# Layer 0 of an image and attention kernel: x for the residual goes into other places, and is biased and turned over at another point

## The chip, the cores and the metric

The kernel runs on one core of a Trainium2 chip. A core has five engines with a queue of instructions each: TensorE (PE; its weight loads are listed as PEld), VectorE (DVE), ScalarE (ACT), GpSimd (POOL) and SyncE (SP). SP issues most of the DMA transfers, which 16 DMA engines carry out. The metric is the device time of one execution in microseconds (us); lower is better. The kernel before took 2713.66 us (median of three runs, 2711.21 to 2717.59).

## The reference, cut to what matters

The input x is an image of 256 channels and 64 x 64 pixels, in float32. Layer 0 normalises it by groups of channels, and adds to x a linear attention over windows of the image. Layer 1, an attention over all pixels and a mixture of eight experts, isn't touched by the change.

```python
x = x + _L0_conv_ref(_gn(x), Wq, Wk, Wv, Wout, bout)      # layer 0

def _L0_conv_ref(x, Wq, Wk, Wv, Wout, bout):              # 8 heads of 32 channels
    q, k, v = projections of x by Wq, Wk, Wv
    q = sigmoid(q); k = sigmoid(k)
    v = v / maximum(norm(v, axis=channels of a head), 1e-12)
    Ik, Ikv = integral images of k and of k * v
    for w in (1, 2, 4):                                   # box of 64 / w pixels
        wk, wkv = _box(Ik, 64 // w), _box(Ikv, 64 // w)
        attn = (q . wkv) / (q . wk + 1e-06)
    return Wout @ concatenate(attn) + bout
```

The sum with x is the residual. The kernel keeps it in the tile `t`, with pixels on the partitions; x comes from memory with channels outermost, so it must be turned over on its way into `t`, and `bout` is added to it before that.

## The kernel before, in words

Layer 0 works on 4096 pixels in 32 tiles of 128 (NT = 32), ordered so that eight strips (NCH = 8) of eight columns hold four bands (NB = 4) of 16 rows each. The 256 channels are handled in two halves (KC = 2, the loop variable `g`): for each half `prepare` (from L393) makes keys, values, sums and queries, and `attend` (from L696) uses them. The change touches `prepare` for g = 0 and what stands ahead of it.

1. **Load and statistics.** Eight DMAs (L324) bring x; DVE takes its statistics (L343) and writes the normalised image to `act` (L358, eight instructions). Statistics, means and some constants lie in a small pool, `c_x`, that ends here.
2. **The rows for the residual.** L369 to L375: the tile `rows` takes the place of x (tag "qk"), so its DMAs wait until the last L358 has read x. Sixteen DMAs on SP's queue, of 256 KB each, load x again: four bands (`b`), each in four quarters (`q`). `biased(b)` (L377) adds `bout` on ACT, eight instructions a band (L379). `residual(b)` (L382) turns a band over on DVE into `t`, eight instructions of 32 x 32 blocks (L385).
3. **Keys and values.** The loop over `i4` (L436) makes eight groups of four tiles. In each: 16 matmuls into a pair of PSUM banks (L441; the trace lists 16 halves for 8 instructions of the program), a sigmoid on ACT into `kt` (L453), a copy on DVE into `v` (L454), squares on POOL (L455), their sums by head on DVE (L456). After the fourth and the eighth group, a square root on ACT (L459) and the normalisation of 16 tiles of `v` on DVE (L460 to L463). The pairs of banks are three in number, shared with the sums of cells. Sigmoid and square root lie in different tables of ACT, so each change loads a table (1.28 us).
4. **Sums of cells.** `sum_cells` (L407), four parts: small matmuls `kt` x `v` (L418) that need the normalised `v`; ACT copies them to the tile `st` (L430). The first two parts are emitted in the last two rounds of the loop, the other two in the next stage.
5. **Area and boxes.** A loop over eight strips `ix` (L530): matmuls of `kt` with a triangular constant (L534, L538), and additions on DVE (L543 to L548). Between them DVE does the steps of `near` (L486): running sums over `st` (L490, L493), then differences (`boxes`, L504 and L510) into tiles `half` and `ssum` for the widths 4 and 2.
6. **Queries and denominators.** `by_channel` (L471) projects queries and keys again by channel (L476), with a sigmoid on ACT (L483). For three widths DVE makes `tall` and `edge` (L583, L585) and the products with the queries (L597 to L604, in two product tiles of the pool's tag "st"), which PE sums (L608). L621 ends the stage, and `attend` follows.

What sets the order: the program's tile framework places the instructions of every engine in a fixed order when the program is built; each engine takes its own queue in that order and waits for semaphores of the others. `tc.issue_after(x)` says that the instructions inside may stand only behind x. Before the change the biasing and the turning over are placed like this:

```python
    if not g and i4 >= NT - 8:                               # groups 6 and 7: bands 0 and 1
        order.enter_context(tc.issue_after(biased((i4 - NT + 8) // 4)))
    ...
    if not g:                                                # after the loop
        biased(2)
        biased(3)
    ...
    if not g and 1 <= ix <= NB:                              # area strips 1 to 4
        with tc.issue_after(latest.ins):
            residual(ix - 1)
```

Of the kernel before, what the change touches and what calls it, by code (L numbers as in the profile page):

```python
# [22 lines left out]
F32 = mybir.dt.float32  # L23
BF16 = mybir.dt.bfloat16
I32 = mybir.dt.int32
AF = mybir.ActivationFunctionType
# [16 lines left out]
D = 32  # L43
GRP = 8
REACH = (4, 2, 1)
# [75 lines left out]
def tile_conv_attn_hybrid(ctx: ExitStack, tc: tile.TileContext, a: dict, out: bass.AP):  # L121
    nc = tc.nc
# [145 lines left out]
    with ExitStack() as phase:  # L268
# [9 lines left out]
        big = phase.enter_context(tc.tile_pool(name="c_big", bufs=1))  # L278
# [18 lines left out]
        with (  # L297
# [21 lines left out]
            x = big.tile([P, KC, N], F32, tag="qk", name="x")  # L319
            xr = a["x"].rearrange("(k p) n -> p k n", p=P)  # L320
            for i in range(4):
                for k in range(KC):
                    at = slice(i * N // 4, (i + 1) * N // 4)
# [42 lines left out]

        rows = big.tile([P, NB, C // D, 4 * IMG], F32, tag="qk", name="rows")  # L369
        for b in range(NB):  # L370
            for q in range(4):
                nc.sync.dma_start(
                    rows[D * q : D * (q + 1), b],
                    a["x"].rearrange("(j c) (b q f) -> b q c j f", c=D, b=NB, q=4)[b, q],
                )  # L375

        def biased(b):  # L377
            for j in range(C // D):
                last = nc.scalar.activation(rows[:, b, j], rows[:, b, j], AF.Identity, bias=bout[:, j : j + 1])  # L379
            return last.ins  # L380

        def residual(b):  # L382

            for i in range(NCH):
                last = nc.vector.transpose(  # L385
                    t[:, NB * i + b, :C].rearrange("p (j c) -> p j c", c=D),
                    rows[:, b].rearrange("p j (y i c) -> p j y i c", y=4, c=SW)[:, :, :, i, :],
                )
            return last.ins

# [2 lines left out]
        def prepare(g, w3, prep, ps):  # L393
# [8 lines left out]
            v = big.tile([P, NT, P], F32, tag="v", name="v")  # L402
            sq = prep.tile([P, NT, P], F32, tag="area", name="sq")
            heads = lambda z: z.rearrange("p i (h d) -> p (i h) d", d=D)
            st = prep.tile([P, NCH, SW, D], F32, tag="st", name="st", bufs=2)
            cells = []

            def sum_cells(part):

                if part % 2 == 0:  # L410
                    cells.append(two_banks())
                sp = cells[-1]
                for i in range(NT // 4 * part, NT // 4 * (part + 1)):
                    for u in range(2):
                        us = slice(CELL * u, CELL * (u + 1))
                        for h in range(4):
                            hs = slice(D * h, D * (h + 1))
                            nc.tensor.matmul(  # L418
                                sp[hs, u, D * (i % 16) : D * (i % 16 + 1)],
                                kt[us, i, hs],  # L420
                                v[us, i, hs],
                                start=True,
                                stop=True,
                                skip_group_check=True,
                            )
                if part % 2:
                    some = slice(NCH // 2 * (part // 2), NCH // 2 * (part // 2 + 1))
                    for u in range(2):
                        with tc.issue_after(rooted.ins):
                            nc.scalar.copy(  # L430
                                st[:, some].rearrange("p i (m u) f -> p i m u f", u=2)[:, :, :, u, :],
                                sp[:, u, :].rearrange("p (i m f) -> p i m f", m=NB, f=D),
                            )

            ss = prep.tile([P, 4 * NT], F32, name="ss")
            for i4 in range(0, NT, 4):  # L436
# [10 lines left out]
                        )  # L447
                at = slice(i4, i4 + 4)

                with ExitStack() as order:  # L450
                    if not g and i4 >= NT - 8:
                        order.enter_context(tc.issue_after(biased((i4 - NT + 8) // 4)))
                    nc.scalar.activation(kt[:, at, :], kv[:, :, 0, :], AF.Sigmoid)  # L453
                nc.vector.tensor_copy(v[:, at, :], kv[:, :, 1, :])  # L454
                nc.gpsimd.tensor_mul(sq[:, at, :], v[:, at, :], v[:, at, :])  # L455
                nc.vector.tensor_reduce(ss[:, 4 * i4 : 4 * (i4 + 4)], heads(sq[:, at, :]), AX.X, ALU.add)  # L456
                if i4 % 16 == 12:
# [5 lines left out]
                    unit_v = nc.vector.tensor_mul(to, to, ss[:, half].unsqueeze(2).to_broadcast([P, 2 * NT, D]))  # L463
                if i4 >= NT - 8:
                    sum_cells((i4 - NT + 8) // 4)

            if not g:
                biased(2)
                biased(3)

            def by_channel(n, i):  # L471

# [13 lines left out]
            def near():  # L486


                for i in range(1, NCH):
                    nc.vector.tensor_add(st[:, i], st[:, i], st[:, i - 1])  # L490
                    yield
                for i in range(1, SW):
                    nc.vector.tensor_add(st[:, :, i], st[:, :, i], st[:, :, i - 1])  # L493
                    yield

                def boxes(to, src, r, axis):
# [16 lines left out]

                for r in REACH[:2]:
                    half = prep.tile([P, NCH, SW, D], F32, tag="st", name="half", bufs=2)
                    boxes(half, st, r, 0)
                    yield
                    boxes(ssum[r], half, r, 1)
                    yield
# [10 lines left out]
            for ix in range(NCH):  # L530
# [18 lines left out]
                side, latest = upto, add  # L549
                if ix in (1, 2):  # L550
                    sum_cells(ix + 1)
                if not g and 1 <= ix <= NB:
                    with tc.issue_after(latest.ins):
                        residual(ix - 1)
                for _ in range(3 if ix > 1 else 0):
                    next(steps, None)
            for _ in steps:
# [1597 lines left out]
```

## Time and profile before

The page describes one profiled execution; the median of the runs comes from other executions of the same kernel.

| | |
|---|---|
| median of three runs | 2713.66 us (2711.21 to 2717.59) |
| the profiled execution's own time | 2709.02 us |
| its span, from first to last instruction | 2707.1 us |
| mean granted clock of TensorE | 0.99 |
| busy share of the span: PE, DVE, ACT, POOL | 97%, 69%, 56%, 30% |
| first preparation of layer 0 (from the first projection to L621) | 22.28 to 127.43 us |
| `rows` DMAs on SP's queue | 16 x 256 KB, issued 27.3 to 39.6 us |
| biasing (L379, ACT) | 32 instructions of 0.50 us, begun between 45.1 and 70.6 us |
| turning over (L385, DVE) | 32 instructions of 0.40 us, begun between 62.5 and 82.1 us |

How to read the views: a line of the order of time gives the start, the length, the engine, the line of the code, the operation, and what it writes and reads; "x8" means that eight such instructions are joined. In brackets stands how long the engine had been idle before and what it waited for. Lines joined this way overlap a little, since an engine starts an instruction before the one ahead has quite ended. A line of stretches gives start and end, the length, then the busy time of each engine with its number of instructions, the granted clock of TensorE, the busy share of the DMA engines and GB/s. The chain of work that ended last is followed back from the last instruction, at each step to what released it.

### The profile page before, as it was taken

What the parts mean: (1) busy time and instruction counts of PE and PEld (TensorE: products, weight loads), DVE (VectorE), ACT (ScalarE), POOL (GpSimd) and SP (SyncE); (2) the same over time, 40 slices, a digit from 0 to 9 for tenths busy, and PEclk for the clock granted to TensorE, in tenths of its full rate; (3) what the DMA queues carried; (4) which work ended last, traced back from release to release, by engine and by line L of the source; (5) the groups of instructions that cost most, each with busy time, mean ns of one, the idle gap of its engine ahead of it and who ended that gap; (6) DMA issues with size and microseconds to landing.
All of it is one profiled execution on the core that took longest, in us unless ns stands there. A gap on an engine that the chain in (4) does not pass through costs nothing.

```text
span 2707.1 us, 70743 instructions
## 1 busy us (share of the span) xinstructions
PE 2624.4 (97%) x30398; PEld 1221.8 (45%) x30398; DVE 1880.5 (69%) x2570; ACT 1518.1 (56%) x2079; POOL 817.9 (30%) x919
## 2 busy tenths in 40 slices
PE   6999999999999999999999999999999999999995
PEld 5465436746544654111212121212121278888884
DVE  6868788586878866888888889888888871111114
ACT  3342323234232435999898989898989842222222
POOL 2067777306777731010000100000001122222220
PEclk9899999999999999999999999999999999999996
DMA  5000000000000000555555555555556645555555
GB/s 148 7 19 26 10 29 22 12 13 23 26 9 31 22 22 13 113 115 118 110 114 114 118 109 118 105 118 118 126 114 151 153 142 197 173 200 170 191 175 196
DMA packets 114461, 256.56 MB, mean 95 GB/s; under 512 B 19890, under 2 KB 76440, under 8 KB 100052
## 3 DMA queue, kind: packets, MB, share of 16 engines
q0 software_dynamic: 22240, 132.66, 23.4%
q1 hardware_dynamic: 84724, 110.30, 12.5%
q10 hardware_dynamic: 7168, 8.92, 1.0%
q8 instruction: 242, 3.96, 0.6%
q14 instruction: 87, 0.71, 0.1%
HBM read 118.64 MB, written 17.86 MB: 50 GB/s over the span
## 4 chain that ended last, share of the span: by engine, by line
PE 91%; DVE 4%; DMA 3%; issue 1%; ACT 1%; POOL 0%; ACTq 0%; SPq 0%; DVEq 0%; POOLq 0%
PE ps_three L1860 19%; PE ps_acc L1819 19%; PE ps_sc L887 8%; PE ps_yp L1528 8%; PE ps_hp L1511 7%; PE ps_acc L903 7%; PE ps_sc L767 3%; PE ps_sc L797 3%; PE ps_acc L841 3%; PE ps_two L441 2%; PE ps_mm L1303 2%; DMA yrows<-v,qk 2%; PE ps_two L534 1%; PE ps_acc L816 1%; PE ps_three L1794 1%; PE ps_mm L1318 1%
## 5 line engine op out<-in xcount | busy, mean ns | idle before, releaser
L1860 PE MATMUL ps_three<-qk 32*64 32x512 f32 x6144 | 563.2, 612 | 2.3 <-DVE t L1798 1.3
L1860 PE MATMUL ps_one<-qk 32*64 32x512 f32 x2048 | 556.3, 613 | 0.2 <-ACT pe L1869 0.2
L1892 DVE TENSOR_TENSOR act<-act,pe 128x2048 f32<-128x2048 f32 x195 | 447.3, 2294 | 82.5 <-ACT pe L1872 51.6
L1872 ACT ACTIVATE pe<-ps_three 128x1536 f32<-128x1536 f32 x330 | 477.3, 1446 | 0.0
L651 ACT COPY sm<-ps_sc 128x384 f32<-128x384 f32 (+2 forms) x418 | 212.9, 539 | 452.4 <-PE ps_sc L887 323.0
L659 DVE TENSOR_TENSOR sm<-ps_sc,mask 128x512 f32<-128x512 f32 (+3 forms) x788 | 343.3, 499 | 64.7 <-PE ps_sc L887 62.3
L659 POOL TENSOR_TENSOR sm<-sm,mask 128x192 f32<-128x192 f32 (+4 forms) x444 | 349.9, 819 | 113.3 <-ACT sm L651 113.2
L1892 DVE TENSOR_TENSOR act<-act 128x2048 f32<-128x2048 f32 x150 | 343.8, 2292 | 51.4 <-ACT act L1872 37.9
L1880 POOL DMA_DIRECT2D pe<-pe x108 | 93.4, 865 | 939.8 <-ACT pe L1872 610.4
L1819 PE MATMUL ps_acc<-pe,v 128*32 128x512 f32 x2640 | 351.6, 604 | 0.0
L1514 ACT ACTIVATE v<-ps_hp,qk 128x256 f32<-128x256 f32 (+1 forms) x256 | 123.1, 481 | 342.6 <-PE ps_hp L1511 342.6
L1860 PEld LDWEIGHTS ps_three<-qk 32*64 32x64 f32 x6144 | 112.6, 129 | 414.5 <-ACT pe L1869 244.0
L1872 ACT ACTIVATE act<-ps_three 128x1536 f32<-128x1536 f32 x182 | 263.1, 1446 | 0.0
L1528 PE MATMUL ps_yp<-qk,v 128*128 128x256 f32 (+1 forms) x1088 | 241.7, 380 | 0.0
L1511 PE MATMUL ps_hp<-qk 128*128 128x256 f32 (+1 forms) x1024 | 236.8, 389 | 2.8 <-ACT v L1514 1.7
L887 PE MATMUL ps_sc<-qk 32*128 32x256 f32 (+5 forms) x3456 | 233.2, 445 | 0.1
L1869 ACT ACTIVATE pe<-ps_one 128x512 f32<-128x512 f32 x330 | 197.5, 598 | 58.3 <-PE ps_one L1860 33.8
L1528 PEld LDWEIGHTS ps_yp<-qk,v 128*128 128x128 f32 (+1 forms) x1088 | 200.3, 187 | 30.7 <-issue 1.3
L903 PE MATMUL ps_acc<-sm,v 128*32 128x256 f32 (+4 forms) x2816 | 211.7, 407 | 0.1
L659 POOL TENSOR_TENSOR sm<-sm,ycut 128x512 f32<-128x512 f32 (+3 forms) x130 | 144.4, 1133 | 214.0 <-ACT sm L651 213.7
L1511 PEld LDWEIGHTS ps_hp<-qk 128*128 128x128 f32 x1024 | 180.7, 189 | 52.7 <-ACT v L1514 12.8
L1819 PE MATMUL ps_acc<-act,v 128*32 128x512 f32 x1456 | 193.9, 604 | 0.0
(364 smaller groups left out, 2908.8 us busy)
## 6 DMA issues: line engine op xcount, KB each, us to landing
pe<-pe POOLq DMA_DIRECT2D x108, 1024.0 KB, 7.6
qk<-in_L_ffn_W SPq DMA_DIRECT2D x64, 1024.0 KB
by<-recs SPq DMA_DIRECT2D x48, 256.0 KB
rows<-in_x SPq DMA_DIRECT2D x16, 256.0 KB
qk<-in_L_ffn_b SPq DMA_DIRECT2D x32, 128.0 KB
y<-yrows SPq DMA_DIRECT2D x8, 512.0 KB
y<-yrows ACTq DMA_DIRECT2D x8, 512.0 KB
rec<-recs SPq DMA_DIRECT2D x60, 64.0 KB
```

The costliest lines, as they stand in the source:

```text
L651: copied = nc.scalar.copy(sm[:, :used], sc[:, :used])
L659: done = engine.tensor_mul(to, of, mk.unsqueeze(1).to_broadcast(list(to.shape)))
L887: nc.tensor.matmul(scs[h][u : u + rows, at : at + n], kT[hs[h], P * i + u : P * i + u + rows], qT[hs[h], CH * ix + CELL * c0 : CH * ix + C ...
L903: nc.tensor.matmul(acc[hs[h], CELL * c0 : CELL * c1], v[:, i, hs[h]], sms[h][:, at : at + n], start=not begun[0], stop=last and at == plac ...
L1511: nc.tensor.matmul(hp[:, :n], w1[:, k, tok(m)], x_now[:, k, :n], start=k == 0, stop=k == KC - 1)
L1514: done["gelu"] = nc.scalar.activation(hid[:, m, :n], hp[:, :n], AF.Gelu, bias=cols[:, m : m + 1]).ins
L1528: product = nc.tensor.matmul(yp[:n], hid[:, m, P * j : P * j + n], w2[:, m, :], start=m == 0, stop=m == NH - 1)
L1819: nc.tensor.matmul(to[D * hd : D * (hd + 1), :], lhsT(hd), rhs(hd), start=start, stop=stop, skip_group_check=True,)
L1860: nc.tensor.matmul(to[CELL * u : CELL * (u + 1), :], qk[hs, 1, g, P * i + CELL * u : P * i + CELL * (u + 1)], qk[hs, 0, g, chunk(qc)], sta ...
L1869: first = nc.scalar.activation(head(pe, 0), one, AF.Exp, scale=C**-0.5)
L1872: nc.scalar.activation(pe[:, CH:], three.rearrange("p h n -> p (h n)"), AF.Exp, scale=C**-0.5).ins
L1892: latest[:] = [nc.vector.tensor_add(total, total, weights_of[r, i]).ins]
```

## The change

It touches only g = 0 of layer 0.

- `rows` is no longer one tile in the place of x, but four, one for each band. Bands 2 and 3 lie in the two places of the tag "st" in the preparation's own pool, which later hold the cell sums, `half` and the products. Bands 0 and 1 lie in the places of `ssum4` and `ssum2`. The DMAs are written down at the head of `prepare`, in the order of bands 2, 3, 0, 1.
- The tile `st` is asked for later, at the first `sum_cells`, so that it follows the rows in the same place.
- `biased` and `residual` move into the loop of keys and values: a band is biased behind the sigmoid of groups 1, 2, 3 and 4, and the next group's sigmoid must stand behind it; it is turned over behind the next group's copy of `v`, and the copy after that must stand behind the turning.
- The former places are empty. The number of DMAs, biasings and turnings is the same.

```diff
-        rows = big.tile([P, NB, C // D, 4 * IMG], F32, tag="qk", name="rows")
-        for b in range(NB):
-            for q in range(4):
-                nc.sync.dma_start(
-                    rows[D * q : D * (q + 1), b],
-                    a["x"].rearrange("(j c) (b q f) -> b q c j f", c=D, b=NB, q=4)[b, q],
-                )
+        rows = {}
+
+        def rows_in(prep):
+            for b, at in ((2, None), (3, None), (0, REACH[0]), (1, REACH[1])):
+                pool, tag, bufs = (big, f"ssum{at}", 1) if at else (prep, "st", 2)
+                rows[b] = pool.tile([P, C // D, 4 * IMG], F32, tag=tag, name="rows", bufs=bufs)
+                for q in range(4):
+                    nc.sync.dma_start(
+                        rows[b][D * q : D * (q + 1)],
+                        a["x"].rearrange("(j c) (b q f) -> b q c j f", c=D, b=NB, q=4)[b, q],
+                    )
...
-            st = prep.tile([P, NCH, SW, D], F32, tag="st", name="st", bufs=2)
+            if not g:
+                rows_in(prep)
+            bands = iter(() if g else (2, 3, 0, 1))
+            turning = []
+            behind_band = {"ACT": nullcontext(), "DVE": nullcontext()}
+            st = []
...
+                if not st:
+                    st.append(prep.tile([P, NCH, SW, D], F32, tag="st", name="st", bufs=2))
...
-                with ExitStack() as order:
-                    if not g and i4 >= NT - 8:
-                        order.enter_context(tc.issue_after(biased((i4 - NT + 8) // 4)))
-                    nc.scalar.activation(kt[:, at, :], kv[:, :, 0, :], AF.Sigmoid)
-                nc.vector.tensor_copy(v[:, at, :], kv[:, :, 1, :])
+                with behind_band["ACT"]:
+                    made = nc.scalar.activation(kt[:, at, :], kv[:, :, 0, :], AF.Sigmoid)
+                with behind_band["DVE"]:
+                    copied = nc.vector.tensor_copy(v[:, at, :], kv[:, :, 1, :])
+                behind_band.update(ACT=nullcontext(), DVE=nullcontext())
+                if turning:
+                    with tc.issue_after(copied.ins):
+                        behind_band["DVE"] = tc.issue_after(residual(turning.pop()))
+                band = next(bands, None) if i4 else None
+                if band is not None:
+                    with tc.issue_after(made.ins):
+                        behind_band["ACT"] = tc.issue_after(biased(band))
+                    turning.append(band)
...
-            if not g:
-                biased(2)
-                biased(3)
-
...
-                if not g and 1 <= ix <= NB:
-                    with tc.issue_after(latest.ins):
-                        residual(ix - 1)
```

More of the change, by code (lines that the diff above doesn't have):

```diff
@@ L365, in tile_conv_attn_hybrid @@
                     )
-        rows = big.tile([P, NB, C // D, 4 * IMG], F32, tag="qk", name="rows")
-        for b in range(NB):
-            for q in range(4):
-                nc.sync.dma_start(
-                    rows[D * q : D * (q + 1), b],
-                    a["x"].rearrange("(j c) (b q f) -> b q c j f", c=D, b=NB, q=4)[b, q],
-                )
+        rows = {}
[8 more added lines that the diff above has]
+                    )
         def biased(b):
             for j in range(C // D):
-                last = nc.scalar.activation(rows[:, b, j], rows[:, b, j], AF.Identity, bias=bout[:, j : j + 1])
+                last = nc.scalar.activation(rows[b][:, j], rows[b][:, j], AF.Identity, bias=bout[:, j : j + 1])
             return last.ins
@@ L386, in residual @@
                     t[:, NB * i + b, :C].rearrange("p (j c) -> p j c", c=D),
-                    rows[:, b].rearrange("p j (y i c) -> p j y i c", y=4, c=SW)[:, :, :, i, :],
+                    rows[b].rearrange("p j (y i c) -> p j y i c", y=4, c=SW)[:, :, :, i, :],
                 )
@@ L430, in sum_cells @@
                             nc.scalar.copy(
-                                st[:, some].rearrange("p i (m u) f -> p i m u f", u=2)[:, :, :, u, :],
+                                st[0][:, some].rearrange("p i (m u) f -> p i m u f", u=2)[:, :, :, u, :],
                                 sp[:, u, :].rearrange("p (i m f) -> p i m f", m=NB, f=D),
@@ L486, in near @@
             def near():
+                (sums,) = st
                 for i in range(1, NCH):
-                    nc.vector.tensor_add(st[:, i], st[:, i], st[:, i - 1])
+                    nc.vector.tensor_add(sums[:, i], sums[:, i], sums[:, i - 1])
                     yield
                 for i in range(1, SW):
-                    nc.vector.tensor_add(st[:, :, i], st[:, :, i], st[:, :, i - 1])
+                    nc.vector.tensor_add(sums[:, :, i], sums[:, :, i], sums[:, :, i - 1])
                     yield
@@ L515, in near @@
                     half = prep.tile([P, NCH, SW, D], F32, tag="st", name="half", bufs=2)
-                    boxes(half, st, r, 0)
+                    boxes(half, sums, r, 0)
                     yield
```

## The prediction

> **What bounds the kernel now.** I read the page first, then the stretches of the stage that changes, then PE, SP, ACT and DVE in order of time. The page:
>
> ```profile
> PE 2624.4 (97%) x30398; PEld 1221.8 (45%) x30398; DVE 1880.5 (69%) x2570; ACT 1518.1 (56%) x2079; POOL 817.9 (30%) x919
> PE 91%; DVE 4%; DMA 3%; issue 1%; ACT 1%; POOL 0%; ACTq 0%; SPq 0%; DVEq 0%; POOLq 0%
> ```
>
> PE has 91% of the chain that ended last, so only what moves PE's work moves the end. The change touches the first preparation (g = 0), some 106 us. Its stretches (length, busy time of PE, PEld, DVE, ACT, POOL, then PE's granted clock and the DMA share):
>
> ```profile
> 22.00:49.00 27.00, 26.72 (x146) 22.95 (x146) 15.79 (x23) 10.07 (x19) 6.07 (x6) 1.00 0.84 155
> 49.00:82.00 33.00, 33.00 (x643) 25.64 (x624) 26.57 (x70) 14.17 (x32) 2.21 (x3) 1.00 0.01 4
> 100.00:128.00 28.00, 22.85 (x68) 5.89 (x64) 25.81 (x27) 5.67 (x8) 0.00 (x0) 0.83 0.05 15
> ```
>
> PE never stops from 22 to 99 us; from 100 to 128 DVE is the full one and PE waits for it. PE in order of time (start, length, what):
>
> ```profile
> 22.28 26.51 PE L441 MATMUL ps_two<-w,act 128*128 128x256 f32 x112 [1.58 <-issue]
> 48.73 1.29 PE L418 MATMUL ps_two<-v,kt 64*32 64x32 f32 x128
> 82.02 17.38 PE L476 MATMUL ps_two<-act,w 128*128 128x512 f32 x40
> ```
>
> Seven groups of projections end at 48.73, the area sums at 82.02, and five groups of L476 at 99.4. SP, ACT and DVE:
>
> ```profile
> 27.27 12.64 SPq L372 DMA_DIRECT2D rows<-in_x  x16
> ```
> ```profile
> 43.29 1.28 ACT L453 ACT_TABLE_LOAD   x1
> 49.33 3.29 ACT L379 ACTIVATE rows<-rows,bout 128x256 f32<-128x256 f32 x8
> ```
> ```profile
> 44.12 2.29 DVE L463 TENSOR_TENSOR v<-v,ss 128x2048 f32<-128x2048 f32 x1
> 62.46 2.72 DVE L385 STREAM_TRANSPOSE t<-rows 128x256 f32<-128x256 f32 x8
> 93.53 2.35 DVE L597 TENSOR_TENSOR prod<-tall,qk 128x1024 f32<-128x1024 f32 x2
> 104.22 1.23 DVE L597 TENSOR_TENSOR prod<-tall,qk 128x1024 f32<-128x1024 f32 x1
> 127.43 0.69 DVE L621 TENSOR_SCALAR rec<-ps_mm 128x512 f32<-128x512 f32 x1 [2.01 <-PE ps_mm L608]
> ```
>
> A band costs ACT 3.3 us and DVE 2.7 us. Today the four turnings stand at 62 to 82 us, where DVE had room and PE did not wait for them; the values v of the first half were normalised (L463) by 46.4, 2.3 us ahead of the cell sums (L418) that read them. The second width's products start at 104.22, and the denominators' sum ends the stage at 127.43.
>
> **What the Trainium skill says.** "TensorE: Matmul & The Clock Gate", Part 1, What's actually happening: the array falls to half clock after an idle window of about 3.4 us and is back after about 3.4 us of sustained work. The trace agrees: 100–128 has a mean granted clock of 0.83 (0.50 between 120 and 132), and from 22 to 26 us 9 matmuls take 3.72 us, while from 28 to 30 eleven fill 2.00 us, some 0.19 each. The same page, Architectural detail: ScalarE and VectorE are strict first-in first-out queues. The trace shows kt (L453) standing behind five L379 from 46.75 to 48.83. "ScalarE: Activation LUTs", What ACT_TABLE_LOAD costs: 1283 ns, plus a drain of some 1380 ns. The trace has 1.28 us and kt directly behind it at 44.58, so I take 1.28.
>
> **The change, part by part.** Times are us from the span's start; group n is the n-th of eight groups of four tiles.
>
> *The load.* Sixteen transfers of 256 KB stay; the places change. In the changed kernel as built, SP's order is: three quarters of band 0, then a wait for the 32nd signal of DVE, which is the last L358, then band 2, band 3, the last quarter of band 0, and band 1. The first bands' place ("st") lies where the statistics' pool was, so it is free only when that pool is done. L358 ends at 27.2, the same moment that SP waits for today. So only 3 of 16 transfers get earlier. Today the sixteenth issue (39.6) waits for the eighth landing; at 200 GB/s in 30–48 us one takes 1.31, so the first lands at 30.4, the fourth at 34.4, the eighth at 39.6. With thirteen left: band 2 at 34.4, band 3 at 39.6, the last quarter of band 0 at 40.9, band 1 at 46.1. The two bias-row DMAs (L937, L938), now behind them on SP, and the second group's weights (issued at 114) are read far later: nothing.
>
> *ACT.* In program order: kt of group 1 at 31.6; band 2 waits for its data: 34.4–37.7; kt of group 2 37.7–38.3 (today 35.0); band 3 again waits for data: 39.6–42.9; kt of group 3 to 43.5; band 0 43.4–46.7; kt of group 4 to 47.3; table load to 48.6, root (0.26) to 48.8. Today that root came at 43.0.
>
> *DVE and POOL.* v of group 3 43.5–44.2 (0.69); turning of band 3 44.2–46.9; then the reduction to 47.6 (its squares on POOL, 1.04, ended at 45.4, hidden); v of group 4 to 48.2; four turnings of band 0 to 49.6; maximum, turning, reciprocal (0.55), turning to 51.0; L463 51.0–53.3. PE's seven groups don't wait: group 6 needs the buffer of group 3, free at 44.2 against 45.3.
>
> *PE.* It reaches the cell sums at 48.7 and must wait for L463: a new gap of 53.3 – 48.7 = 4.6. Both parts of sums (2 x 1.22) and the last group (3.65) end at 59.4, today 54.8. (That group needs v of group 5. Group 6's kt is put ahead of band 1: table load to 50.1, kt to 50.7, band 1 to 54.0, kt to 54.6, v to 55.3; PE is there at 55.8, so it hides by 0.5.) The second half's normalisation ended 6.6 after the last group (53.6, 60.2); now 66.0. PE has two area steps of 6.2 before it needs that: 65.6. So the third part of sums starts at 66.1, today 61.07: PE is 5.0 later, and the area ends at 87.0.
>
> *What comes back.* The 32 turnings (4 x 2.72 = 10.9) leave DVE between 62 and 82, so the sums of cells and boxes no longer stand behind the area. Today the second width starts 104.22 – 82.02 = 22.2 behind the area. Then: 1.9 of box sums, 2.3 of tall, products and edges end 16.4 behind it; but the second width needs a product buffer that PE frees after its five L476 groups and four L608, 17.4 + 1.0 = 18.4. What is late next is thus PE, and of 10.9 only 3.8 come back. From there the same 21.2 of DVE work (104.22 to 125.42), plus 0.9 of wait for the other buffer, which now comes behind one more L476 group (3.45). Net recovery 2.9. Sum: 5.0 – 2.9 = +2.1.
>
> *The clock.* The trace of before has no gap of 4.6 inside this stage, so bound it. No fall: 0. At worst two windows of 3.4 at half clock lose 3.4. I take the loss seen at 22 us: 3.72 – 9 x 0.19 = 2.0. Forecast +4.1, bounds +2.1 and +5.5. Below nothing I exclude for the clock: a gap can't raise a clock of 1.00.
>
> Behind the stage every engine's order is that of before, instruction for instruction, and PE is the bound, so the shift is carried to the end one to one.
>
> **Sum.** The profiled execution took 2709.0 (span 2707.1 and 1.9 around it), 4.6 under the median of the three runs shown, 2713.66 (they spread over 6.4). Same execution: 2713.1. Median: 2713.66 + 4.1 = 2717.8, +0.15%. About 0.2% (5.4 us) is what a measurement of this kernel can tell from no change.
>
> **Rivals.**
> 1. *Half clock holds* (22%). PE at half speed behind the gap may not count as busy enough to rise: at 118.7–132.4 it stayed low for four windows (13.7 us). Against it: there PE kept waiting, here it is fed. Price: 6.8 lost, 2.1 + 6.8 = +8.9, 2722.6. It is slower by my bound from a loss of 3.3 on.
> 2. *The load does come early, as the words say* (8%): then bands start at 32.2, the gap is 1.0, but the last group waits 1.9 for group 5 behind band 1, whose queue is then the bound; PE 3.2 late, 2.9 back: +0.3, 2714.0. Against it: the wait on L358.
> 3. *PE's gap closes* (10%), if ACT's and DVE's steps overlap more than their rows show: only the recovery is left, –2.9, 2710.8. Against it: two landings (34.4, 39.6) that ACT can't pass. Even this is no 0.2%.
>
> **How the numbers follow.** Forecast 60%, centre 2717.8; its own range with a median's scatter of about 2 is 2713.5–2721. Low end 2712 takes in rival 2 and the upper half of rival 3; high end 2722.5 takes in about half of rival 1; some 18% are left out. Slower by over 0.2% (above 2719.1): a fifth of the forecast's cases, in its upper bound with scatter (0.12), and most of rival 1 (0.17), 0.29. Faster by over 0.2% (below 2708.2): only rival 3 with a lucky median, 0.06. Within: 0.65.
>
> **What would show it.** Three L378 issues near 16–17.5 us and the rest from 27.3; ACT waiting for rows twice; the first half's normalisation (now L484) ending near 53; PE idle some 4.6 us before the first cell sums, with a clock of 0.5 behind; turnings gone from 62–82; the area's end near 87 to 89, and DVE waiting for PE before the second width. Wrong would be: PE without a gap near 49 us, or all rows landed by 40 us; or a shift that is not carried past 130 us.

## The result, and the profile after

The changed kernel took 2720.90 us, the median of ten runs (2718.49 to 2727.03); the kernel before beside it took 2713.26 (ten runs, 2706.63 to 2717.59). The ratio is 1.0034, with a 95% interval of 1.0022 to 1.0047: slower by 6 to 13 us. The profiled execution is the slowest of its ten (2727.03, span 2725.2), so the whole span isn't compared below, but the stage, up to the start of DVE's L636 (L621 in the kernel before), the last sum of the denominators.

Lines moved: L372 is now L378, L379 L385, L385 L391, L418 L431, L441 L454, L453 L464, L454 L466, L460 and L463 L481 and L484, L476 L493, L597 L612, L608 L623.

The page of the changed kernel, its busy times and its chain by engine:

```profile
PE 2638.9 (97%) x30398; PEld 1231.9 (45%) x30398; DVE 1880.6 (69%) x2570; ACT 1517.0 (56%) x2079; POOL 815.7 (30%) x919
PE 90%; DVE 4%; DMA 3%; ACT 1%; issue 1%; POOL 0%; SPq 0%; ACTq 0%; DVEq 0%; POOLq 0%
```

DVE and ACT do the same work as before; PE is busy 14.5 us longer with the same 30398 matmuls. The granted clock fits that: ahead of the program's last 50 us it is halved for 44.4 us in this profile, for 13.7 in that of before (the windows are listed among the experiments). By stretches (length, then busy time of PE, PEld, DVE, ACT and POOL, the granted clock, the DMA share and GB/s):

```profile
22.00:49.00 27.00, 26.91 (x111) 23.21 (x112) 17.22 (x36) 14.39 (x33) 4.99 (x5) 1.00 0.73 134
49.00:64.00 15.00, 9.48 (x276) 7.70 (x275) 9.49 (x21) 5.58 (x12) 2.28 (x3) 0.66 0.01 3
64.00:91.50 27.50, 26.78 (x385) 20.39 (x383) 20.89 (x47) 6.83 (x11) 1.04 (x1) 1.00 0.01 2
109.00:134.20 25.20, 21.98 (x72) 5.82 (x64) 21.19 (x22) 4.47 (x5) 0.00 (x0) 0.86 0.06 17
```

Nearly all the damage is in 49 to 64: PE is idle for 5.5 of 15 us and the clock is 0.66. Before, PE had no idle time there, and the last group stood between the two parts of the first half's cell sums:

```profile
49.95 3.72 PE L441 MATMUL ps_two<-w,act 128*128 128x256 f32 x16
53.60 1.29 PE L418 MATMUL ps_two<-v,kt 64*32 64x32 f32 x128
```

PE with the change, in order of time:

```profile
22.09 27.36 PE L454 MATMUL ps_two<-w,act 128*128 128x256 f32 x112 [1.58 <-issue]
52.90 2.60 PE L431 MATMUL ps_two<-v,kt 64*32 64x32 f32 x233 [3.45 <-DVE v L484]
57.56 0.44 PE L431 MATMUL ps_two<-v,kt 64*32 64x32 f32 x23 [2.07 <-issue]
57.93 5.81 PE L454 MATMUL ps_two<-w,act 128*128 128x256 f32 x16
70.51 1.28 PE L431 MATMUL ps_two<-v,kt 64*32 64x32 f32 x128 [0.72 <-DVE v L484]
91.46 17.38 PE L493 MATMUL ps_two<-act,w 128*128 128x512 f32 x40
```

Two things stand between 49 and 64: the forecast wait for L484 (3.45), and a second stop that nobody forecast, 2.07 us in the midst of the cell sums, with no releaser ("issue": the profile shows nothing that PE waited for). The last group then takes 5.81 us instead of 3.72. The area ends at 91.46, against 82.02: 9.44 later. SP, ACT and DVE:

```profile
16.15 1.59 SPq L378 DMA_DIRECT2D rows<-in_x  x3
16.15 19.84 SPq L378 DMA_DIRECT2D rows<-in_x  x16
```
```profile
34.74 3.30 ACT L385 ACTIVATE rows<-rows,bout 128x256 f32<-128x256 f32 x8 [1.93 <-POOL sq L476]
39.78 3.30 ACT L385 ACTIVATE rows<-rows,bout 128x256 f32<-128x256 f32 x8 [1.26 <-DMA rows<-in_x]
43.47 3.29 ACT L385 ACTIVATE rows<-rows,bout 128x256 f32<-128x256 f32 x8
48.54 0.26 ACT L480 ACTIVATE ss<-ss 128x64 f32<-128x64 f32 x1
```
```profile
50.50 2.25 DVE L484 TENSOR_TENSOR v<-v,ss 128x2048 f32<-128x2048 f32 x1
109.90 1.22 DVE L612 TENSOR_TENSOR prod<-tall,qk 128x1024 f32<-128x1024 f32 x1 [1.92 <-PE ps_mm L623]
134.19 0.69 DVE L636 TENSOR_SCALAR rec<-ps_mm 128x512 f32<-128x512 f32 x1 [1.86 <-PE ps_mm L623]
```

The first line of SP is the stretch up to 18 us alone: three transfers are issued early, the fourth at 27.21. ACT's first band waits at 34.74. The releaser named there is POOL's sq (done at 34.66), which a band doesn't read; ACT's queue had stood until 34.47 at its wait for the band's transfers. The second width's products start 109.90 – 91.46 = 18.4 behind the area (22.2 before), and the stage ends at 134.19, 6.8 later than before's 127.43. So 2.7 of 9.4 came back.

### The profile page after: what moved, and what is told of

The parts are those of the page before. It is cut to its first block, busy times and chain, and to the rows that moved or that the text cites. A ratio compares the mean times of both kernels' runs of the same rounds, so it can differ in the third digit from the quotient of the medians.

```text
span 2725.2 us, 70745 instructions
## 1 busy us (share of the span) xinstructions
PE 2638.9 (97%) x30398; PEld 1231.9 (45%) x30398; DVE 1880.6 (69%) x2570; ACT 1517.0 (56%) x2079; POOL 815.7 (30%) x919
## 4 chain that ended last, share of the span: by engine, by line
PE 90%; DVE 4%; DMA 3%; ACT 1%; issue 1%; POOL 0%; SPq 0%; ACTq 0%; DVEq 0%; POOLq 0%
PE ps_three L1875 19%; PE ps_acc L1834 19%; PE ps_sc L902 8%; PE ps_yp L1543 8%; PE ps_hp L1526 7%; PE ps_acc L918 7%; PE ps_sc L782 3%; PE ps_sc L812 3%; PE ps_acc L856 3%; PE ps_mm L1318 2%; DMA yrows<-v,qk 2%; PE ps_two L493 2%; PE ps_acc L831 1%; PE ps_two L552 1%; PE ps_two L454 1%; PE ps_three L1809 1%
## 5 line engine op out<-in xcount | busy, mean ns | idle before, releaser
L1884 ACT ACTIVATE pe<-ps_one 128x512 f32<-128x512 f32 x330 | 197.3, 598 | 59.4 <-PE ps_one L1875 34.8
L1526 PEld LDWEIGHTS ps_hp<-qk 128*128 128x128 f32 x1024 | 181.1, 189 | 53.3 <-ACT v L1529 11.9
```

The costliest lines, as they stand in the source:

```text
L1526: nc.tensor.matmul(hp[:, :n], w1[:, k, tok(m)], x_now[:, k, :n], start=k == 0, stop=k == KC - 1)
L1884: first = nc.scalar.activation(head(pe, 0), one, AF.Exp, scale=C**-0.5)
```

## The experiments

The theory at the outset: the moved steps hold up L484; PE's wait for it, a stall in the cell sums and the halved clock behind them make the loss; the earlier second width gives part of it back. The rivals are named in each expectation. All times are from the profile of the kernel in question; the stage's end is the one from above. In the prediction and the expectations the eight groups are numbered from 0; ordinals here count from the first.

```
kernel                 first cell sums  area ends  stage ends   ratio to before [95%]
before (3 profiles)    48.6 to 49.4     81.9-82.7  127.3-128.1
the change             52.90            91.46      134.19       1.0034 [1.0022, 1.0047]
the change, again      53.01            90.83      132.83       1.0037 [1.0022, 1.0052]
steps only             55.87            95.12      137.13       1.0036 [1.0025, 1.0047]
early load             50.40            87.87      130.55       1.0013 [0.9996, 1.0030]
gap filled             53.04            90.77      133.63       1.0029 [1.0020, 1.0038]
sums apart             53.30            89.12      131.12       1.0019 [1.0002, 1.0036]
bias only              51.93            95.31      139.52       1.0046 [1.0032, 1.0059]
earlier bands          57.89            93.26      135.26       1.0029 [1.0019, 1.0039]
early load, apart      48.81            88.08      130.95       1.0008 [0.9998, 1.0017]
two in the loop        48.07            84.72      126.72       1.0017 [1.0008, 1.0027]
two, and later         48.49            81.85      123.86       0.9993 [0.9981, 1.0005]
```

The ratios of many of these kernels lie within each other's intervals, so the argument rests on the stage. That is one profile for each kernel, two of the change and three of before.

**Steps only.** The rows in x's old place, the steps where the change puts them:

```diff
-                pool, tag, bufs = (big, f"ssum{at}", 1) if at else (prep, "st", 2)
-                rows[b] = pool.tile([P, C // D, 4 * IMG], F32, tag=tag, name="rows", bufs=bufs)
+                rows[b] = whole[:, b]       # whole: one tile, tag "qk"
```

> Rows lie in one tile in x's old place again, loaded behind the last normalisation of x as in the kernel before; the biasing and turning stay where the change put them. Theory (the moved steps cost, the new places and the load do not): band 2 is there at about 34.4 us, band 3 at 39.6, bands 0 and 1 some 4 us later than with the change (44.8 and 50.1), so the last turning in the loop ends at 54 to 56 instead of 52.75, the first cell sums start at 53 to 56, and the area sums end at 91 to 95 us against 82.0 before and 91.5 with the change. Rival (the load into the new places is what costs): the area sums end at 82 to 85 and the time is within 0.1% of before.

PE of this kernel:

```profile
55.87 2.62 PE L431 MATMUL ps_two<-v,kt 64*32 64x32 f32 x234 [7.41 <-DVE v L466]
60.52 0.43 PE L431 MATMUL ps_two<-v,kt 64*32 64x32 f32 x22 [2.03 <-issue]
```

The area ends at 95.12, just past the end of the range. The wait that ended last isn't for L484, though, which was done at 52.66: it is for a copy L466 (55.12 to 55.81), which frees one of the three pairs of banks for the sums. That copy's sigmoid (54.51) stood behind band 0 on ACT (51.32). The moved steps bring the loss without the new places; the places and the earlier load are worth 3.7 us at the area's end, on the good side. In the time the two kernels can't be told apart (1.0036, 1.0034). The rival, that the load into new places costs, fell.

**Early load.** What kept the "st" places back was the pool of the statistics. Its small tiles go elsewhere:

```diff
-            mv = small.tile([P, KC, 2], F32, name="mv")
+            mv = wts.tile([P, KC, 2], F32, name="mv")
```
(and so for mean, off and rstd)

> The change, with the small tiles of x's statistics moved to another pool, so that the rows' places are free behind the statistics (about 21 us) and not behind the last normalisation (27.2). Theory (the late landing of the bands holds the loop's end up): band 2 is there at about 28 us, 3 at 33, 0 at 34.5, 1 at 40; all four bands are biased and turned without a wait for a transfer, the gap on TensorE ahead of the first cell sums shrinks from 3.45 us to under 1.5, the clock isn't halved there, the area sums end at 82 to 85 us and the time is 2711 to 2715 (ratio 1.000). Rival (ScalarE's and VectorE's queues alone make the gap, whenever the bands land): the gap stays 3 us or more and the area sums end at 89 or later, ratio 1.003. Second rival (the transfers take the memory from x's own load or the projections): bands land later than 5 us behind the start of each.

```profile
50.40 2.17 PE L431 MATMUL ps_two<-v,kt 64*32 64x32 f32 x234 [0.93 <-DVE v L466]
54.50 0.32 PE L431 MATMUL ps_two<-v,kt 64*32 64x32 f32 x22 [1.92 <-issue]
54.75 5.41 PE L454 MATMUL ps_two<-w,act 128*128 128x256 f32 x16
```

ACT no longer waits for a transfer and the wait ahead of the sums is 0.93: that half of the theory holds, and the rival fell. What is left of the wait isn't for L484, which ended at 47.66, before PE was there (49.47). It is again for a copy L466 (49.66), whose sigmoid stood behind band 0 and a table load on ACT (44.43 to 49.0). But the area ends at 87.87, not at 82 to 85: with the gap gone, the stall of 1.92 stayed, and the clock fell at 55.1 behind it. A stall with almost no wait ahead of it is a cause of its own.

**Gap filled.** Four matmuls of 128x512 whose result nobody uses, behind the seventh group: added work.

```diff
+                    with tc.issue_after(projected.ins):
+                        for j in range(4):
+                            fill = nc.tensor.matmul(spare, w3[:, 0, 0, :], act[:, 0, chunk(j)], start=True, stop=True)
```

> The change, with four 128x512 matmuls whose result nobody uses on TensorE behind the projections of the seventh group and ahead of the first cell sums: added work that fills the gap. Theory (the gap's length is set by VectorE's turning, and about 4.4 of the 9.4 us come from TensorE running at half clock and a stall behind it): VectorE's turning of the last band in the loop still ends at 52.5 to 53, the clock stays full from 28 to past 62 us, the last group's projections take 3.65 us instead of 5.81, and the area sums end 2 to 4.5 us earlier than with the change (87 to 89.5 us); the time is 2 to 4 us below it. Rival (the clock falls for another reason, such as the small matmuls of the cell sums): the clock is halved near 52 to 62 us all the same, and the area sums end at 91 or later.

```profile
49.19 3.60 PE L490 MATMUL ps_mm<-act,w 128*128 128x512 f32 x8
53.04 2.08 PE L431 MATMUL ps_two<-v,kt 64*32 64x32 f32 x225 [0.25 <-DVE v L484]
57.36 0.35 PE L431 MATMUL ps_two<-v,kt 64*32 64x32 f32 x31 [2.24 <-issue]
57.65 5.41 PE L454 MATMUL ps_two<-w,act 128*128 128x256 f32 x16
```

Stretch of 54 to 58 us, the clock in the third column from the right:

```profile
54.00:58.00 4.00, 1.76 (x168) 1.60 (x155) 3.59 (x11) 0.51 (x2) 1.04 (x1) 1.00 0.02 4
```

Half a miss. The sums start when L484 lets them, as before, and the clock stays full through the filled gap, so the gap is what dropped it at 52.0 in the change. But the stall came at full clock, as long as ever (2.24), and dropped the clock at 58.5 for one window of 3.4 us; the area ends only 0.7 earlier than with the change (0.1 than with its second profile). So the stall isn't a consequence of the halved clock; the clock fell behind the stall.

**Sums apart.** With the change, both parts of the first half's cell sums stand ahead of the last group; in the kernel before, the second part stands behind it. Put back:

```diff
                 if i4 >= NT - 8:
-                    sum_cells((i4 - NT + 8) // 4)
+                    with tc.issue_after(projected.ins):
+                        sum_cells((i4 - NT + 8) // 4)
```

> The change, with the second part of the cell sums held behind the last group's projections, where it stands in the kernel before (with the change both parts, 512 small matmuls, stand back to back ahead of that group). Theory (TensorE's stall of 2.07 us with no wait in the record, within the second part, is the fetch of instructions that small matmuls use up faster than they come): no such stall of over 1 us is left, a 0.3 to 1 us wait takes its place ahead of the last group or none, and the area sums end 1 to 2 us earlier than with the change, at 89.5 to 90.5. Rival (the stall belongs to the halved clock or the values it reads): a stall of about 2 us stays in the second part, and the area sums end at 91 or later.

```profile
53.30 1.54 PE L431 MATMUL ps_two<-v,kt 64*32 64x32 f32 x128 [3.88 <-DVE v L484]
55.55 5.21 PE L454 MATMUL ps_two<-w,act 128*128 128x256 f32 x16 [0.72 <-DVE v L466]
60.69 1.29 PE L431 MATMUL ps_two<-v,kt 64*32 64x32 f32 x128
```

No stall, in either part, though the clock was halved from 51.8 to 58.6; a wait of 0.72 took its place. The area ends at 89.12, 2.3 earlier than with the change. (A part is 64 matmuls of the program, which the profile counts as 128 records; both are 256 records, so the 512 of the expectations is too many. The stall came behind record 225 to 234 of 256, in all five kernels that ran the parts in one row, and in none that didn't.) That in this preparation the stall comes with the row of both parts, and goes when they are parted, is shown.

A single part isn't safe everywhere, however. In the second preparation (g = 1), where no two parts stand in a row in any of these kernels, the fourth part stalls in thirteen of fourteen profiles, those of before among them:

```profile
536.80 1.24 PE L418 MATMUL ps_two<-v,kt 64*32 64x32 f32 x123
539.65 0.26 PE L418 MATMUL ps_two<-v,kt 64*32 64x32 f32 x5 [1.61 <-issue]
```

That the stall is the fetch of instructions is argued, not shown by an experiment. The trace of the change has a transfer of 16 KB of kind "instruction" at 54.97 that took 1.35 us, and the stall ends 1.25 us behind that. All nineteen stalls in the cell sums, of both preparations and all profiles, end 1.24 to 1.43 us behind the end of such a transfer. With the sums apart the transfer (55.31, 1.08 us) falls beside the last group's larger matmuls, which don't stop.

**Bias only.** The rows in x's old place, biased in the loop, turned beside the area as in the kernel before:

```diff
-                if turning:
-                    with tc.issue_after(copied.ins):
-                        behind_band["DVE"] = tc.issue_after(residual(turning.pop()))
...
+                if not g and 1 <= ix <= NB:
+                    with tc.issue_after(latest.ins):
+                        residual(ix - 1)
```

> Rows in one tile in x's old place, loaded as in the kernel before; the biasing stands in the loop as the change puts it, the turning stands beside the area sums as before. Theory A (VectorE's turning in the loop is what ends last ahead of the first cell sums): without it the square roots of the first half are worked on by 48.5 to 49 us, the scaling of the first half of v ends at 51 to 52 and the area sums end 1.5 to 4 us earlier than with the steps moved alone (95.1), at 91 to 93.5; the turnings then cost the second width's start what they cost before, so the stage ends 6 to 8 us later than before. Theory B (ScalarE's biasing in its queue ahead of the sigmoids and the square root, and the bands' late landing, set the gap alone): the area sums end at 94.5 to 95.5 as with the steps moved alone. The kernel's ratio to before is 1.002 to 1.004 either way.

```profile
51.93 2.31 PE L431 MATMUL ps_two<-v,kt 64*32 64x32 f32 x234 [3.19 <-DVE v L466]
```
```profile
62.28 0.60 ACT L464 ACTIVATE kt<-ps_two 128x512 f32<-128x512 f32 x1 [8.57 <-PE ps_two L454]
62.78 3.29 ACT L385 ACTIVATE rows<-rows,bout 128x256 f32<-128x256 f32 x8
65.97 0.58 ACT L464 ACTIVATE kt<-ps_two 128x512 f32<-128x512 f32 x1
```

The normalisation of v's first half ended at 51.3 and the sums start 3.9 earlier than with all steps in the loop (55.87). Only 1.4 of that is the normalisation, which ended at 52.66 there. The rest is in the copy L466 that PE waits for: here it stands right behind the normalisation (51.19), there behind a sigmoid that stood behind band 0. The framework had put the steps of ACT and DVE in another order, so how much of the 7.4 us gap is the turnings' own stays open.

Behind that the run tells nothing, for the same reason. The sigmoid at 62.28 starts the moment the eighth group's projections end. Band 1 stands behind it, and behind band 1 the next sigmoid (65.97). By the edit the sixth group's sigmoid must stand behind band 1, so this can only be the sixth's, whose projections were done before 48.7: the framework put the eighth group's sigmoid ahead of it in ACT's queue. So the area's end (95.3) speaks for neither theory.

**Earlier bands.** Early load, and the bands spread over other groups:

```diff
+            bias_behind, turn_behind = ({}, {}) if g else ({0: 2, 4: 3, 8: 0, 20: 1}, {4: 2, 8: 3, 24: 0})
```

> The change with the rows' places free behind the statistics, the bands biased behind groups 0, 1 or 2, 2 to 4 and 5 (bands 2, 3, 0, 1), band 2 turned behind v of group 1, band 3 behind group 2 or 3, band 0 behind group 6, and band 1 beside the area sums as before. Theory (what the change loses is the wait ahead of the first cell sums, the stall in 512 cell sums in a row and the clock behind them; what it gains is the second width's earlier start): the scaling of the first half of v ends by 49 us, the first cell sums start within 0.5 us of the last projection before them, no stall of over 1 us, full clock to past 80 us, the area sums end at 81.5 to 83.5 us, the second width starts within 19.5 us of that, and the time is 1 to 3 us below before (ratio 0.9985 to 1.000; 5 to 10 us below the change). Rival (the work moved into the loop delays the sums wherever it stands): the area sums end at 85 or later and the ratio is 1.001 or more.

```profile
21.93 19.28 PE L453 MATMUL ps_two<-w,act 128*128 128x256 f32 x80 [1.58 <-issue]
42.63 7.39 PE L453 MATMUL ps_two<-w,act 128*128 128x256 f32 x32 [1.41 <-DVE v L465]
57.89 1.54 PE L430 MATMUL ps_two<-v,kt 64*32 64x32 f32 x128 [7.87 <-ACT rows L385]
```
```profile
41.26 0.60 ACT L463 ACTIVATE kt<-ps_two 128x512 f32<-128x512 f32 x1 [9.50 <-PE ps_two L453]
41.75 3.29 ACT L385 ACTIVATE rows<-rows,bout 128x256 f32<-128x256 f32 x8
44.94 0.58 ACT L463 ACTIVATE kt<-ps_two 128x512 f32<-128x512 f32 x1
```

A failure, and by the same trap: the sigmoid at 41.26 starts as five groups of projections end (21.93 + 19.28 = 41.21). By the edit the third group's sigmoid must stand behind band 3, which is biased only now (41.75). So the one at 41.26 is the fifth group's, put ahead of band 3 in ACT's queue, and the third's is the one at 44.94, though its projections were done two groups, some 7 us, before 41.21. Everything behind is late. In the kernels that follow, no sigmoid ahead of the first cell sums stands behind one that waits for a later group's projections.

**Before and the change once more.** The same two kernels, for what varies from one execution to another:

> The kernel before once more, with a profile, for what varies between two executions. Theory (the halved clock in the attention, in windows of 3.41 us, comes and goes by execution and belongs to no kernel): this execution shows one or more such windows in the attention (150 to 2660 us) that the first one didn't have, or the next execution of the change lacks some of its three; the order and length of everything up to the area sums' end at 82.0 us are within 0.3 us of the first. Rival (those windows are the change's own, set off by its different start): none in the attention here.

> The change once more, with a profile. Theory (windows of halved clock in the attention vary by execution): the area sums end within 1 us of 91.5 with the 2.07 us stall and the halved clock near 52 to 62 us there again, while the windows at 137 to 151, 192 to 199 and 663 to 670 us are not all there again or lie elsewhere. Rival (they belong to the change): all are there at the same places, and the shift against before grows from 6.8 us at the stage's end to about 18 at the program's end again.

Windows of halved clock, us from the span's start, to 700:

```
before           118.7-132.4
before, again    118.6-132.2, 589.6-596.4
the change       52.0-62.2, 127.0-133.9, 137.3-150.9, 191.9-198.7, 662.9-669.8
the change again 54.2-61.0, 136.1-139.5, 187.3-194.1, 549.1-552.5
```

The stage is the same again: stall 2.12, area ends at 90.83 and 81.92. The windows behind it aren't: of the change's three behind its stage, one came back much shorter, one near its place, one elsewhere. The shift against before, taken at equal VectorE instructions, goes from 6.8 at the stage's end to 18.1 at the program's end in the first profile, from 5.4 to 14.0 in the second. A single profile against a single profile thus says little past the stage.

**Early load and sums apart together.**

> Early load and sums apart together: the rows' places free behind the statistics, and the second part of the cell sums behind the last group's projections. Theory (the change's loss is made of the wait ahead of the first cell sums, the stall in 512 cell sums in a row, and the clock that falls behind either): the wait stays at about 1 us as with the early load alone, no stall of over 1 us is left in the sums, the clock stays full or falls for one window at most, the area sums end at 83.5 to 86.5 us (82.0 before, 87.9 with the early load alone, 89.1 with the sums apart alone), the stage ends 0 to 2.5 us earlier than before and the ratio is 0.999 to 1.001. Rival (the two cures act on the same time, so that together they give no more than either alone): the area sums end at 87 to 88 and the ratio is 1.001 to 1.002.

```profile
48.81 1.29 PE L431 MATMUL ps_two<-v,kt 64*32 64x32 f32 x128 [0.92 <-DVE v L466]
52.97 6.76 PE L454 MATMUL ps_two<-w,act 128*128 128x256 f32 x16 [2.86 <-DVE v L466]
```

The stall is gone and the wait ahead of the sums is 0.92. But the last group now stands right behind the first part, and meets a wait that the stalled row had hidden: 2.86 us for the buffer of the sixth group, whose v starts at 52.22, behind band 0's turning on DVE (48.67 to 51.39) and behind the same group's sigmoid, which stood behind band 1 on ACT (51.61). The clock falls within that wait, at 52.3. The area ends at 88.08: as the rival said, the two cures bring no more than one, though for another reason than that they act on the same time.

**Two in the loop.** So, on top of both cures, fewer steps ahead: only band 2 ahead of the first square root, bands 3 and 0 biased and turned behind it, band 1 turned beside the area:

```diff
+            bias_behind, turn_behind = ({}, {}) if g else ({4: 2, 16: 3, 20: 0, 24: 1}, {8: 2, 20: 3, 24: 0})
```

> As early load and sums apart together, with fewer of the moved steps ahead of the first cell sums: band 2 is biased behind the sigmoid of group 1 and turned behind v of group 2, band 3 is biased behind the square root of the first half, bands 0 and 1 behind groups 5 and 6, bands 3 and 0 turned behind v of groups 5 and 6, band 1 beside the area sums. Theory (only what stands ahead of the scaling of v's first half on ScalarE and VectorE delays the first cell sums): that scaling ends at 45 to 47 us, the first cell sums start with no wait of over 0.3 us, the clock is full from 28 to past 100 us, the area sums end at 82 to 83.5 us, the stage ends 1 to 2.5 us earlier than before, and the ratio is 0.999 to 1.0002. Rival (sigmoids that wait for a later group's projections, as in the earlier bands' kernel, or the queue of the second half hold the area sums up): the third part of the cell sums starts at 64 us or later (61.1 before) and the ratio is 1.001 or more.

```profile
62.32 1.41 PE L430 MATMUL ps_two<-v,kt 64*32 64x32 f32 x128 [1.77 <-DVE v L481]
```

The first sums have no wait, the third part has one of 1.77, behind a second half that still had a bias and a turning in its queue; the clock falls at 63.0 for one window. The stage ends 0.7 earlier than before, but the time is a miss: 1.0017, where 0.999 to 1.0002 was expected. The area's end, 84.72, lies past its range too.

**Two, and later.** Band 1's bias behind the second square root, bands 0 and 1 turned beside the area:

```diff
+            bias_behind, turn_behind = ({}, {}) if g else ({4: 2, 16: 3, 20: 0}, {8: 2, 20: 3})
...
+            if not g:
+                with tc.issue_after(rooted.ins):
+                    biased(1)
```

> As the kernel with two bands in the loop, with less in the second half's queue too: band 1 is biased behind the second square root, and bands 0 and 1 are turned beside the area sums; bands 2 and 3 stay turned in the loop. Theory (the 1.77 us wait ahead of the third cell sums, and the halved clock window behind it, came from the turning of band 0 and the biasing of band 1 ahead of the last sigmoid): no wait of over 0.5 us ahead of the third cell sums, which start at 60.5 to 61.5 us, full clock from 28 to past 110, area sums' end at 81 to 82.5 us, the stage's end 1 to 3 us earlier than before (124.5 to 126.5 against 127.4). If the attention behind it runs as in before, the ratio is 0.9985 to 1.000. Rival (a kernel with the early start of its second width meets halved clock in the attention more often, as the two-in-loop kernel did): stage as above, ratio 1.001 or more, with a window of 6.8 us some 90 to 100 us behind the area sums' end.

```profile
48.49 1.29 PE L430 MATMUL ps_two<-v,kt 64*32 64x32 f32 x128
49.77 3.72 PE L453 MATMUL ps_two<-w,act 128*128 128x256 f32 x16
53.42 1.29 PE L430 MATMUL ps_two<-v,kt 64*32 64x32 f32 x128
60.90 1.29 PE L430 MATMUL ps_two<-v,kt 64*32 64x32 f32 x128
81.85 17.38 PE L495 MATMUL ps_two<-act,w 128*128 128x512 f32 x40
```
```profile
123.86 0.69 DVE L641 TENSOR_SCALAR rec<-ps_mm 128x512 f32<-128x512 f32 x1 [1.14 <-PE ps_mm L628]
```

PE has no wait up to the area's end, as in the kernel before, and the clock is full from 25.9 to 176.1. There the window came that the rival named, some 94 us behind the area's end, but not the rival's ratio. The second width's part keeps its gain: 123.86 – 81.85 = 42.0, against 45.4 before. The stage ends 3.6 earlier. The time is 0.9993 of before [0.9981, 1.0005]: no gain over before can be claimed, since the interval holds 1; against the change it is some 11 us faster, by the two ratios (1.0034 – 0.9993 = 0.0041). The two turnings that stayed beside the area cost nothing there (two in the loop, with one, has the same 42.0).

**The kernel before, a third time.**

> The kernel before a third time. Theory (halved clock in the attention at 170 to 200 us depends on what runs ahead of it, and the kernel before doesn't meet it): none between 133 and 500 us, as in its first two executions. Rival (it comes by chance in about half of all executions of any of these kernels): one of 3.4 to 6.8 us between 170 and 200 us.

The theory fell. The third profile of before has halved clock from 181.5 to 191.7, longer than the rival's 3.4 to 6.8 us and worth 4.8 us. The kernel before meets it too.

## Why the prediction was right, and where its sum was off

The sign, the place and the wait for L484 were right; 2720.9 lies 3.1 above the 2717.8 forecast and within the range. The size was not: the shift is 7.6 us against 4.1, past the sum's own bounds (+2.1 and +5.5). That the range holds it is owed to the room left for rival 1 and for scatter, so in that it was lucky. The outcome called likeliest, within 0.2% of before, did not come (1.0034). By its steps:

- *The load*: three transfers early, the rest behind the last L358; bands at 34.7, 39.8 and 43.5 on ACT (forecast 34.4, 39.6, 43.4). Right, and the kernel with the early load shows that the landings mattered.
- *ACT and DVE*: the root at 48.54 (48.6), L484 ended at 52.75 (53.3). Right, half a microsecond too long. PE's wait was 3.45, not 4.6, partly because the projections ended at 49.45: the clock first rose at 28.1 in this execution, at 26.5 in that of before. The sums' start moved by 52.90 – 48.73 = 4.2 (4.6).
- *The step that failed* is "Both parts of sums (2 x 1.22) and the last group (3.65) end at 59.4", the 6.1 us behind the gap. They took 63.58 – 52.90 = 10.7. Of the 4.6 more, 2.07 is the stall, 2.00 the last group at half clock (57.93 to 63.58 is 5.65, less 3.65), and 0.5 the sums at half clock. The clock's term was put at 2.0 and measured 2.5; the stall was no term at all. I had read that both parts now stand in one row, and priced the row at twice one part. Sums apart and gap filled show that the row has a price of its own at either clock.
- *Behind it*: the third part of sums waited 0.7 more. Sum at the area's end: 4.17 + 4.59 + 0.68 = 9.44, forecast 7.0.
- *What comes back*: the second width 18.4 behind the area, as worked out; 45.41 – 42.73 = 2.7 recovered (2.9). Kernels with no halved clock in that part need 42.0, that is 3.4 back.
- *Carried one to one*: the stage's shift is 9.44 – 2.68 = 6.8 us, or 1.0025, inside the interval (6.0 to 12.8 us). The profiled execution alone would have misled: it ends 18.1 later. With most of the other kernels the stage's shift lies within the ratio's interval as well. The change's second profile lies just outside (5.4 us, interval from 6.0). Two in the loop is the clear exception: its stage is 0.7 earlier, its time 2 to 7 us longer. Chance windows in the attention (its profile has one at 179.0 to 185.9, which cost 3.2) may be why; that isn't shown.
- *Rivals*: "half clock holds" came true in its sign (three windows, 10.2 us) and not in its price of 6.8, since PE was idle or in short matmuls for much of that time. Its reason isn't shown, since the stall lies within those windows. What the prediction held against it, that PE is fed here, is no safeguard (see the last section). "PE's gap closes" is what the last kernel built on purpose: no wait, and a stage 3.6 shorter (forecast 2.9). "The load does come early" was put at +0.3 and measured +3.1 at the stage's end. Its gap of 1.0 was right in number (0.93) but not in what was waited for, a pair of banks instead of L484. Its wait of the last group for the sixth group's v showed once the parts were parted (2.86; it said 1.9). The stall and the clock behind it were missing again.

Open is whether the stall is instruction fetch (no run here takes the fetch away by itself), why nearly every second preparation has one too, and what sets off the windows in the attention.

## What to carry to other kernels

Before work is moved into an engine's slack, ask which instruction behind it in the queue releases the busiest engine: here a root and a multiply of 2.5 us decided, and steps that cost nothing behind them cost 9 us of the area's end ahead of them. A gap on PE costs its length and then the clock, so price both; and look at what the scheduler put side by side as a result, since two short runs of small matmuls in one row had a stall here that neither had alone. Where an engine starts exactly as a later group ends, look whether that group's step was put ahead of the others in the engine's queue.

## What the runs showed of the hardware

- A row of 256 records of 64x32 matmuls stalled for 1.92 to 2.24 us behind record 225 to 234, at full and at half clock alike (six of six profiles). Rows of 128 did not in the first preparation; in the second, the last of four did for 0.83 to 1.67 us, in thirteen of fourteen profiles. Each of these stalls ended 1.24 to 1.43 us behind a 16 KB transfer of kind "instruction".
- The clock fell in windows of 3.41 us, for one to four of them ahead of the program's last 50 us. All fifteen PE gaps of 1.9 us and more between 30 and 135 us, in nine of the fourteen profiles, had halved clock around or behind them. The Trainium skill ("TensorE: Matmul & The Clock Gate", Part 1, What's actually happening) puts the fall behind an idle window of about 3.4 us; here shorter gaps were enough. That holds for the fall at 118.7 in before too, which the prediction read as agreeing with the section: the gaps around it were 1.76 and 1.83 us. Gaps of that length had a fall in or behind them in some kernels and none in others (two, and later, at 115 to 121). In the attention, a gap of 1.3 us, 91 to 97 us behind the area's end, had halved clock for 6.8 to 10.2 us behind it in seven of thirteen profiles. The same section calls the window free-running, so that it matters where in it a gap lies; that would fit, and no run here shows it.
- Work does not always bring the clock back after 3.4 us, as the prediction took it from that section. In the third profile of before PE was busy for all of 10.25 us at half clock (length, PE's busy time, clock, DMA share and GB/s):

```profile
181.45:191.70 10.25, 10.25 (x136) 0.50 0.01 2
```
